# First row blocks' weights by ScalarE's queue, two products between mixed row blocks, mixing in accumulator banks

## The chip, the cores and the metric

The kernel runs on one core of one Trainium2 chip. The metric is the device time of one execution in microseconds (us); the number compared is the median of several runs. A profiled execution of the same kernel gives the page and the trace that this text reads. Engines are named as the profile names them: PE is TensorE's matmul, PEld its weight load, DVE is VectorE, ACT is ScalarE, POOL is GpSimd, SP is SyncE, which issues most of the transfers.

## The reference

Inputs are `x` (32 batches, 64 channels, 1024 positions), one condition number out of 16 for each batch, and a table of sixteen 64 x 64 mixing matrices. A two-layer network of width 4096 follows, and its result is added to `x`:

```python
W = weights[condition]                      # (32, 64, 64)
y = einsum('bct,bcd->bdt', x, W)            # mixing of channels, per batch
h = gelu(einsum('bsd,df->bsf', y, inter_w) + inter_b)
out = x + einsum('bsf,fd->bsd', h, output_w) + output_b
```

Everything is float32. The two matrix products of the network are the bulk of the work; the mixing is a small piece at the beginning.

## The kernel before

**Mixing.** Two batches make one row block of 128 partitions (2 x 64 channels); there are 16 row blocks. The function `mix` multiplies, for each of 8 slices of 128 positions and for each of the two batches, a 64 x 128 piece of `x` (the stationary operand) with the 64 x 64 weights of that batch. That is 16 matmul instructions, which the profile records as 32 matmuls and 32 weight loads, as each float32 instruction is executed in two passes. The results lie in PSUM, and `mixed` copies them into Y, the left operand of the network, half by ScalarE and half by VectorE. Tiles named `x` hold row blocks of the input, `wsel_e` their mixing weights, `py` the PSUM results. Ten row blocks are mixed before the products begin (in the order 2, 3, 6, 7, 0, 1, 4, 5, 8, 9), six more later, between products (tile `pl`, function `mix_later`).

**Weights of the mixing.** `start_rows` loads the condition numbers and works out a table row for each partition. `gather` then fetches the weights of one row block by an indirect transfer of GpSimd's queue; there are ten of these at the beginning.

**The products.** Both network products are done by two nested levels of a Strassen-Winograd scheme: seven products of quarter matrices (`OUTER`), each of them by seven products of quarters of those (`INNER`). An inner product is four matmul instructions (eight passes of 256 columns), accumulated in PSUM tiles of tags A, B and C, two buffers each (`psacc`). `product` issues it, `read` adds the result into SBUF tiles (`fX`, `fV`, `fD`). The operands other than plain quarters are sums: of the weights, by GpSimd (`outer_w1`, `inner_w1`), and of Y, by `right_sums`, in which ScalarE copies one operand into PSUM (pool `pst`, tag t) and VectorE adds. The first product of all, fA, takes block (0,0) of quarter 11 of Y and of the weights; the second, fB, takes block (1,0) of the same quarter of Y. Of Y both need only row blocks 0 and 1.

**Order.** Nothing is scheduled by a planner: each step is registered by `at(time, function)`, and all steps are issued in the order of these times, in units of one inner product. Each engine executes its instructions in that order. `MIX` is the distance of row blocks in these units. x is loaded into six buffers (`xpool`), so the seventh load waits for the first mixed block. SP issues first the condition numbers, then six row blocks of x, then the first quarter of the weights (`load_w1(0, "11")`), then four more row blocks as buffers come free, then the other three quarters of the weights.

**PSUM.** Before the products, mixing has its own pool `psx`, three buffers of two banks each; `end_mix` closes it and opens the accumulator pool in its place. `warm` fills TensorE's first microseconds with matmuls of zeros: 24 instructions of 256 columns.

Of the kernel before, what the change touches and what calls it, by code (L numbers as in the profile page):

```python
# [9 lines left out]
F32 = mybir.dt.float32  # L10
# [3 lines left out]
PSUM = bass.MemoryType.PSUM  # L14
# [8 lines left out]
LEFT = {1: "11", 2: "12", 3: "s4", 4: "22", 5: "s1", 6: "s2", 7: "s3"}  # L23
RIGHT = {1: "11", 2: "21", 3: "22", 4: "t4", 5: "t1", 6: "t2", 7: "t3"}
# [51 lines left out]
def kernel(  # L76
# [35 lines left out]
    nc = tc.nc  # L112
    P = 128
# [9 lines left out]
    W = 256  # L123
# [43 lines left out]
    row_c = early.tile([P, NR], I32, name="row_c")  # L167
    wsel_e = early.tile([P, NR - NL, D], F32, name="wsel_e")
    pst = ctx.enter_context(tc.tile_pool(name="pst", bufs=2, space=PSUM))
    psx_ctx = ctx.enter_context(ExitStack())  # L170
    psx = psx_ctx.enter_context(tc.tile_pool(name="psx", bufs=3, space=PSUM))
    late = {}

# [2 lines left out]
    def at(time, fn, *args):  # L178
        steps.append((time, len(steps), fn, args))
# [57 lines left out]
    def blk(q, a, b):  # L237

        return q[:, 2 * a : 2 * a + 2, ts(b, W)]

    def lblk(q, a, b):

        return blk(q, b, a)
# [15 lines left out]
    def wsel(i):  # L259
        return wsel_e[:, i, :] if i < NR - NL else wsel_l[:, i - (NR - NL), :]  # L260

    def gather(i):
# [4 lines left out]
            in_offset=bass.IndirectOffsetOnAxis(ap=rows[:, i : i + 1], axis=0),  # L267
        )


    XT = {}

    FIRST = (2, 3, 6, 7, 0, 1, 4, 5)

    def load_x(i):
        XT[i] = xpool.tile([P, T], F32, tag="x0", name=f"x0_{i}")
# [2 lines left out]
    def warm():  # L279


        z = misc.tile([P, 3 * P], F32, tag="m8", name="zeros")
        nc.vector.memset(z, 0.0)
        for n in range(2):
            t = psx.tile([P, 2, NK, D], F32, tag="py", name=f"warm{n}")
            t = t.rearrange("p j k d -> p (j k d)")
            for _ in range(12):
                nc.tensor.matmul(  # L288
                    t[:, :W], z[:, :P], z[:, P:], start=True, stop=True
                )  # L290

    Y = {}
    Y_ORDER = ("11", "21", "t2", "t3", "t4", "12", "22")
# [6 lines left out]
    YS = {}  # L300
    PY = {}

    def mix(i, out=None):
        if out is None:
            py = psx.tile([P, 2, NK, D], F32, tag="py", name=f"py{i}")
            out = [py[:, j] for j in range(2)]
        for k in range(NK):
            for j in range(2):
                half = slice(j * C, (j + 1) * C)
                nc.tensor.matmul(  # L310
                    out[j][:, k, :],
                    XT[i][half, ts(k, P)],
                    wsel(i)[half, :],
                    start=True,
                    stop=True,
                )
        PY[i] = out
# [22 lines left out]
        YS[i] = t[:, 1, :].rearrange("p (k n) -> p k n", k=NK)  # L340
        nc.sync.dma_start(XT[i], x_rows[i])

    def mix_later(i):
        tiles = [pst.tile([P, 2, W], F32, tag="t", name=f"pl{i}_{j}") for j in range(2)]
        mix(i, [t.rearrange("p a (k d) -> p (a k) d", d=D) for t in tiles])

    def mixed_later(i):
        for j in range(2):
            o = YS[i][:, :, ts(j, D)]
# [20 lines left out]

    def end_mix():
        x0.close()
        psx_ctx.close()
        late["yib"] = right1.enter_context(
            tc.tile_pool(name="yib", bufs=3, side="right", reuse_waits="tile")
        )
        late["acc"] = ctx.enter_context(
            tc.tile_pool(name="psacc", bufs=2, space=PSUM, reuse_waits="tile")
        )


    def outer_y0(a, b):
        return lambda: {
            n: blk(Y[0, n], a, b)
            for n in ("11", "12", "21", "22", "t1", "t2", "t3", "t4")
        }
# [26 lines left out]
    def inner_y(a, p):  # L413
        q = Y[a, RIGHT[p]]
        pool = yia if p in (1, 2) else late["yib"]
        t = lambda n: pool.tile([P, 2, W], F32, tag=f"yi{p}", name=f"y{n}_{a}_{p}")
        YI[a, p] = {
            "11": blk(q, 0, 0),
            "21": blk(q, 1, 0),
            "22": blk(q, 1, 1),  # L420
            "12": blk(q, 0, 1),
            "t1": blk(q, 0, 1),
            "t2": t("i2"),
            "t3": t("i3"),
            "t4": t("i4"),
        }
        return YI[a, p]
# [28 lines left out]
    def inner_w1(it, p):  # L456
# [21 lines left out]
            "s4": s4,  # L478
        }


    LAST = 7 * NH * NG - 1
    state = {}
# [28 lines left out]
    def plan_block(base, unit, blkno, key, nm, mm, operands):  # L512

        last = {}
        for q in INNER:
            slot = q[0]
            if blkno == LAST and slot == 11:
                slot = 7.5
            at(base + slot * unit, product, blkno, q, nm, mm, operands)
            at(base + (slot + 1) * unit, read, blkno, key, q, nm)  # L520
            last[q[4]] = base + (slot + 1) * unit
        return last
# [145 lines left out]
    at(-61, warm)  # L668
    at(-60, start_rows)
    order = FIRST + (8, 9)  # L670
    for j, i in enumerate(order):
        at(-50 + 0.1 * j, gather, i)
    for n in Y_ORDER:
        at(-45, new_y, 0, n)
    MIX = 1.15
    t0 = -len(order) * MIX - 0.7
    for j, i in enumerate(order):
        t = t0 + j * MIX
        at(-40 + 0.1 * j if j < 6 else t0 + (j - 6) * MIX + 1.5, load_x, i)
        at(t, mix, i)  # L680
        at(t + MIX + 0.4, mixed, i)
    at(t0 + 10 * MIX + 1, store_y1, 8)
    at(-39.45, load_w1, 0, "11")
    for j, n in enumerate(("12", "21", "22")):
        at(t0 + 3 * MIX + 1.6 + 0.1 * j, load_w1, 0, n)
    at(-1, lambda: nc.sync.dma_start(b1, inter_b.rearrange("(f p) -> p f", p=P)))
    at(t0 + 10 * MIX + 0.42, end_mix)
    ty = t0 + 4 * MIX + 1.5
    right_sums(ty, outer_y0(0, 1))
    right_sums(ty + 2.3, lambda: inner_y(0, 1))  # L690
    for j, (n, b) in enumerate(((0, 0), (1, 0), (1, 1))):
        right_sums(ty + 4.6 + 2.3 * j, outer_y0(n, b))
    right_sums(ty + 11.5, lambda: inner_y(0, 2))
    for j, p in enumerate((6, 7, 4, 5, 3)):
        right_sums(7 * (j + 2) - 4.5, lambda p=p: inner_y(0, p))
    later = (11.6, 13.9, 21.8, 26.2, 33, 46.6)
    for j, t in enumerate(later):
        i = NR - NL + j
        at(7.5 + 3 * j, gather, i)
        at(max(t - 6, later[j - 2] + 3.3 if j > 1 else 2), load_later, i)  # L700
        at(t, mix_later, i)
        at(t + 1.4, mixed_later, i)
        at(t + 3.2, store_later, i)

# [8 lines left out]
    for it in range(nit):  # L713
# [4 lines left out]
                at(b0 - 49 + t, load_w1, it, n)  # L718
        for n, t in W_AT.items():
            if it == 0:  # L720
                t = {1: -10, 2: -6.8, "s3": -4, "s1": -3}.get(n, t)
            if isinstance(n, str):
                at(b0 + t, outer_w1, it, n)
            else:
                at(b0 + t, inner_w1, it, n)
        for o, p in enumerate(OUTER):
            b = b0 + 7 * o
            plan_block(
                b, 1, 7 * it + o, (it, p), "f", mm1,
                lambda l, r, it=it, p=p, a=a: (WI[it, p][l], YI[a, p][r]),  # L730
            )
            fin = STATE[p][1]
            if fin is not None:
                hidden(b, it, fin)
            if it == NG:
                at(b - 49 + 13, load_y1, Y_ORDER[o])
                right_sums(b - 49 + 20, lambda p=p: inner_y(1, p), gap=0.8)
# [417 lines left out]
```

## Time and profile before

| what | value |
|---|---|
| median of three runs | 1366.71 us (1366.69 to 1367.29) |
| the profiled execution | 1367.58 us |
| its span on the core | 1365.8 us |
| PE busy | 1347.9 us, 99% of the span |
| mean granted clock of TensorE | 0.987 |
| first mixed block begins | 13.86 us |
| first product begins | 49.59 us |
| third product (the first fC) begins | 55.05 us (chain of waits) |

The span is the time from the first to the last instruction that the profile records; the profiled execution's own time is 1.8 us longer. Times of single instructions are counted from the start of the span. A line such as `PE py L310 x32` reads: TensorE, writing tile py, from line 310 of the kernel, 32 records. The granted clock is the share of its full clock that TensorE was given.

### The profile page before, as it was taken

To read this page: it belongs to the slowest core of one execution; us is meant where nothing else is said; L and a number is where in the kernel's file an instruction comes from. 1 tells how busy PE (TensorE), PEld (TensorE's weight loads), DVE (VectorE), ACT (ScalarE), POOL (GpSimd) and SP (SyncE) were. 2 spreads that over 40 slices of the span, in tenths; PEclk is the share of its full clock that TensorE was granted. 3 is DMA by queue.
4 is the path that set the end of the run, shared out by engine and by line. 5 is a ranking of instruction groups with operands and counts; after the bars stand their busy time and mean duration, and the time that the engine had idled before them with its cause. 6 is when DMAs were issued, how large, how long until landed. Compare 5 with 4: busy or idle time off the path is not lost.

```text
span 1365.8 us, 19025 instructions
## 1 busy us (share of the span) xinstructions
PE 1347.9 (99%) x6568; PEld 1182.9 (87%) x6568; DVE 883.3 (65%) x1581; ACT 488.9 (36%) x985; POOL 962.0 (70%) x601
## 2 busy tenths in 40 slices
PE   8999999999999999999999999999999999999998
PEld 8988888888888888888888888888888888888887
DVE  1656557565697665756657575675766757767676
ACT  1433324234354252532524332432433323333341
POOL 4762864957749678396672985958959689496792
PEclk7799999999999999999999999999999999999999
DMA  6455577676898767676668227074270732916611
GB/s 221 135 164 198 175 235 277 232 248 220 301 355 284 232 219 248 244 231 226 230 206 313 95 96 290 18 292 168 79 291 1 266 127 103 358 41 233 245 48 62
DMA packets 135216, 273.40 MB, mean 200 GB/s; under 512 B 15440, under 2 KB 67920, under 8 KB 123472
## 3 DMA queue, kind: packets, MB, share of 16 engines
q1 hardware_dynamic: 134336, 271.53, 57.4%
q8 instruction: 53, 0.87, 0.2%
q0 software_dynamic: 512, 0.53, 0.1%
q14 instruction: 43, 0.35, 0.1%
q10 hardware_dynamic: 272, 0.13, 0.0%
HBM read 167.28 MB, written 104.86 MB: 199 GB/s over the span
## 4 chain that ended last, share of the span: by engine, by line
PE 92%; DVE 4%; issue 1%; ACT 1%; POOL 1%; DMA 1%; DVEq 0%; ACTq 0%
PE fA L527 26%; PE zA L538 24%; PE fC L527 13%; PE zC L538 12%; PE fB L527 6%; PE zB L538 6%; PE py L310 2%; PE tp L1011 1%; DVE hs L187 1%; PE warm L288 1%; PE pl L310 1%; POOL w2p L187 1%; DVE fX L187 1%; DVE fV L187 0%; DMA hs_d<-fD 0%
## 5 line engine op out<-in xcount | busy, mean ns | idle before, releaser
L527 PE MATMUL fA<-yi,wi 128*128 128x256 f32 x896 | 212.5, 380 | 2.5 <-DVE fD L187 1.1
L187 DVE TENSOR_TENSOR hs<-h,t 128x512 f32<-128x512 f32 x308 | 200.5, 681 | 7.0 <-ACT t L207 2.9
L538 PE MATMUL zA<-hs,wt 128*128 128x256 f32 x840 | 197.8, 379 | 0.0
L187 POOL TENSOR_TENSOR h<-h,h 128x1024 f32<-128x1024 f32 x84 | 196.1, 2360 | 1.1 <-DMA h<-hs_d 0.9
L527 PEld LDWEIGHTS fA<-yi,wi 128*128 128x128 f32 x896 | 169.4, 190 | 28.1 <-DVE fX L187 1.9
L538 PEld LDWEIGHTS zA<-hs,wt 128*128 128x128 f32 x840 | 158.4, 190 | 20.9
L187 POOL TENSOR_TENSOR wi<-w 128x512 f32<-128x512 f32 x80 | 101.8, 1272 | 43.8 <-PE fC L527 24.5
L552 ACT ACTIVATE fD<-fD,b 128x256 f32<-128x256 f32 x128 | 58.2, 503 | 186.4 <-DVE fD L187 185.5
L187 POOL TENSOR_TENSOR ws<-w,w 128x1024 f32<-128x1024 f32 x32 | 74.8, 2359 | 68.6 <-PE fA L527 58.3
L207 ACT COPY t<-h 128x512 f32<-128x512 f32 x140 | 82.0, 591 | 74.2 <-DVE hs L187 69.9
L207 ACT COPY t<-hs 128x512 f32<-128x512 f32 x112 | 65.6, 589 | 108.5 <-DVE hs L187 108.5
L187 POOL TENSOR_TENSOR wt<-v 128x512 f32<-128x512 f32 x35 | 44.6, 1275 | 82.3 <-DMA v<-w_d 69.8
L187 DVE TENSOR_TENSOR fX<-fA,fX 128x512 f32<-128x512 f32 x104 | 71.6, 688 | 46.6 <-PE fA L527 46.5
L187 POOL TENSOR_TENSOR wi<-w,wi 128x512 f32<-128x512 f32 x40 | 50.9, 1273 | 63.8 <-PE fA L527 57.1
L527 PE MATMUL fC<-y,wi 128*128 128x256 f32 x384 | 91.0, 380 | 0.1
L527 PEld LDWEIGHTS fC<-y,wi 128*128 128x128 f32 x384 | 72.7, 190 | 10.4 <-issue 0.5
L538 PE MATMUL zC<-hs,v 128*128 128x256 f32 x336 | 79.5, 379 | 1.3 <-ACT mX L921 1.3
L527 PE MATMUL fA<-yi,w 128*128 128x256 f32 x320 | 75.6, 379 | 0.0
L538 PE MATMUL zA<-h,wt 128*128 128x256 f32 x320 | 75.6, 379 | 0.0
L538 PEld LDWEIGHTS zC<-hs,v 128*128 128x128 f32 x336 | 63.7, 190 | 10.2 <-ACT mX L921 1.7
L187 POOL TENSOR_TENSOR wt<-v,wt 128x512 f32<-128x512 f32 x35 | 44.5, 1272 | 33.7 <-PE zA L538 33.7
L538 PEld LDWEIGHTS zA<-h,wt 128*128 128x128 f32 x320 | 60.8, 190 | 8.3
(182 smaller groups left out, 2840.1 us busy)
## 6 DMA issues: line engine op xcount, KB each, us to landing
h<-hs_d SPq DMA_DIRECT2D x56, 1024.0 KB, 7.0
w<-in_L_ffn_inter_w_dram SPq DMA_DIRECT2D x32, 1024.0 KB, 6.8
hs_d<-hs SPq DMA_DIRECT2D x96, 256.0 KB, 3.1
v<-w_d SPq DMA_DIRECT2D x21, 1024.0 KB, 9.3
hs_d<-fD SPq DMA_DIRECT2D x64, 256.0 KB, 3.4
w2p<-in_L_ffn_output_w_dram SPq DMA_DIRECT2D x32, 512.0 KB, 5.0
w_d<-w2p SPq DMA_DIRECT2D x64, 256.0 KB, 2.8
w_d<-w2t SPq DMA_DIRECT2D x48, 256.0 KB, 6.7
```

What stands on the lines that cost most here:

```text
L187: eng.tensor_tensor(o, a, b, ALU.subtract if sub else ALU.add)
L207: nc.scalar.copy(t, src)
L288: nc.tensor.matmul(t[:, :W], z[:, :P], z[:, P:], start=True, stop=True)
L310: nc.tensor.matmul(out[j][:, k, :], XT[i][half, ts(k, P)], wsel(i)[half, :], start=True, stop=True,)
L527: nc.tensor.matmul(acc[:, u, :], lt[:, k, ts(u, P)], rt[:, k, :], start=start and u == 0 and k == 0, stop=k == 1, skip_group_check=True,)
L538: nc.tensor.matmul(acc, wl[:, k, :], hr[:, k, :], start=start and k == 0, stop=k == NG - 1, skip_group_check=True,)
L552: nc.scalar.activation(t[:, u, :], t[:, u, :], AF.Gelu_apprx_tanh, bias=b1[:, f : f + 1])
L1011: nc.tensor.transpose(tp[:, v, ts(n0, P)], d[:, n0, ts(v, P)], late["ident"])
```

## The change

Four things change together.

1. A new function `first_rows` fetches the mixing weights of row blocks 0 and 1. ScalarE loads the four condition numbers into registers and issues four transfers of 64 x 64 numbers, each at an address that a register gives. These two blocks are mixed first, and GpSimd gathers weights only from the third block on.
2. The first two products, fA and fB, are issued after the third mixed block, ahead of the other seven. Their operands are taken straight from Y and from the loaded weights (`y_block`, `w1_block`), as the sums are not made yet.
3. Mixing writes into the accumulator tiles of tags C and B in turn, two tiles for a row block. The pool `psx` is gone, and `mix_later` is merged into `mix`.
4. The warm-up is 26 instructions of 128 columns instead of 24 of 256. The first quarter of the weights is loaded after two row blocks of x instead of after six. The sums of Y come in another order (first those of quarter 11 itself, `inner_y(0, 1)`, then the outer ones), and one of them, t1, gets a tile of its own. Some times of later steps are shifted.

```diff
+    acc_pool = ctx.enter_context(tc.tile_pool(name="psacc", bufs=2, space=PSUM))
...
+    def first_rows(n):
+        _, idx = nc.values_load_multi_w_load_instructions(
+            cond[None, : 2 * n], engines=[mybir.EngineType.Activation],
...
+        for i in range(n):
+            for j in range(2):
+                nc.scalar.dma_start(
+                    wsel(i)[j * C : (j + 1) * C, :],
+                    cond_w[bass.ds(idx[2 * i + j], 1), :, :].rearrange("s c d -> (s c) d"),
+                )
...
-    FIRST = (2, 3, 6, 7, 0, 1, 4, 5)
+    NF = 2
+    FIRST = (0, 1, 2, 3, 6, 7, 4, 5)
...
-        for n in range(2):
-            t = psx.tile([P, 2, NK, D], F32, tag="py", name=f"warm{n}")
...
-            for _ in range(12):
+        t = acc_pool.tile([P, 2, W], F32, tag="A", name="warm")
+        for _ in range(26):
+            nc.tensor.matmul(t[:, 0, :P], z[:, :P], z[:, P:], start=True, stop=True)
...
-            py = psx.tile([P, 2, NK, D], F32, tag="py", name=f"py{i}")
+        pool = acc_pool if tag else pst
+        tiles = [
+            pool.tile([P, 2, W], F32, tag=tag or "t", name=f"py{i}_{j}") for j in range(2)
+        ]
...
+            if blkno == 0 and slot < 2:
+                slot += t0 - 2
...
+    at(-60, first_rows, NF)
-    for j, i in enumerate(order):
+    for j, i in enumerate(order[NF:]):
         at(-50 + 0.1 * j, gather, i)
-    MIX = 1.15
-    t0 = -len(order) * MIX - 0.7
+    MIX = 1.06
+    NB = 3
+    t0 = 2 - (len(order) - NB) * MIX
+    M_AT = {i: t0 + (j - NB) * MIX - (2 if j < NB else 0) for j, i in enumerate(order)}
...
+        at(t, mix, i, "CB"[j % 2])
...
-    at(-39.45, load_w1, 0, "11")
+    at(-39.85, load_w1, 0, "11")
...
+    right_sums(M_AT[3] + MIX + 0.5, lambda: inner_y(0, 1))
+    ty = M_AT[7] + MIX + 0.8
+    for j, (n, b) in enumerate(((0, 1), (1, 1), (0, 0))):
+        right_sums(ty + 2.3 * j, outer_y0(n, b))
+    right_sums(ty + 6.9, lambda: inner_y(0, 2))
+    right_sums(ty + 9.2, outer_y0(1, 0))
...
-    later = (11.6, 13.9, 21.8, 26.2, 33, 46.6)
+    later = (12.5, 14.3, 21.8, 26.2, 33, 46.6)
```

The order on TensorE is then: warm-up; row blocks 0, 1, 2; fA, fB; row blocks 3, 6, 7, 4, 5, 8, 9; the first fC and the rest of the products as before. On SP the order is: condition numbers, x of blocks 0 and 1, the first quarter of the weights, x of blocks 2, 3, 6 and 7, then 4, 5, 8 and 9 as buffers come free, then the other quarters of the weights.

## The prediction, made before the changed kernel was run

> **What bounds the kernel now.** I read the busy shares first, then the clock row of the slices, then the chain of waits from 0 to 60 us, then the windows on PE.
>
> ```profile
> PE 1347.9 (99%) x6568; PEld 1182.9 (87%) x6568; DVE 883.3 (65%) x1581; ACT 488.9 (36%) x985; POOL 962.0 (70%) x601
> ...
> PEclk7799999999999999999999999999999999999999
> ...
> q8 instruction: 53, 0.87, 0.2%
> ```
>
> TensorE is busy 99% of the span, so only less TensorE time, or a faster clock for it, can pay. The clock row has its only low digits in the first two slices (34 us each). The chain there is TensorE alone:
>
> ```profile
> 1.33 12.61 PE warm L288 x48
> 13.93 2.15 PE py L310 x35
> 16.08 1.12 issue
> 17.20 0.44 PE py L310 x3
> 17.64 1.67 issue
> 19.30 30.35 PE py L310 x281
> 49.66 3.67 PE fA L527 x8
> 53.32 1.73 PE fB L527 x8
> 55.05 1.73 PE fC L527 x8
> ```
>
> Warm-up to 13.9, one mixed row block (32 matmuls), a stop of 3.2 us, then nine blocks in 30 us, then the products. fA, the same work as fB, takes 3.67 against 1.73 us. The windows say why; columns are sum, busy us, clock, DMA share, GB/s:
>
> ```profile
> 13.90:16.00 2.10, 2.10 (x36) 1.00 0.65 215
> 16.10:19.30 3.20, 0.44 (x3) 0.96 0.09 26
> ...
> 25.80:29.20 3.40, 3.40 (x36) 0.50 0.49 154
> ...
> 46.30:49.60 3.30, 3.30 (x32) 0.50 0.00 0
> 49.60:53.20 3.60, 3.60 (x10) 0.51 0.43 147
> 53.20:54.90 1.70, 1.70 (x10) 1.00 0.95 283
> ```
>
> After the stop the clock is 0.50 and stays there through 30 us of unbroken mixing; it comes back only 3.5 us into the products. A block costs 3.41 us at 0.50 (ScalarE's copies of consecutive blocks start at 25.80 and 29.21). At 1.00 it costs 1.93: the first later block runs from 70.52 to 72.45 in the timeline. So about 9 x 1.48 = 13.3 us of the mixing, and 1.9 us of fA, are clock.
>
> **What the Trainium skill says.** "TensorE: Matmul & The Clock Gate", Part 1, has the clock halved after about one idle window of 3.4 us and restored after one busy window. The trace agrees on both steps (0.50 after the stop, 1.00 after 3.5 us of products), but adds that mixing matmuls, busy all the time on 64 of 128 rows, do not count as busy enough to restore it. Whether they count as idle enough to lose it from 1.00, neither says: before has no stretch of 3.4 us of mixing alone at 1.00. This is the open question. "Runtime: NRT & Kernel Launch", Instruction fetch mechanics, has blocks of 16 KiB, 256 instructions, fetched by DMA, and a stall after a branch. The trace agrees: queue 8 moved 0.87 MB in 53 packets, 16 KB each, and its first packet comes inside the stop[...].
>
> **The change part by part**, on TensorE's clock of before (span 1365.8, the profiled execution 1367.58, the median 1366.71; I sum differences on the profiled one and take them from the median, 0.9 us apart).
>
> Warm-up. 24 matmuls of 256 columns (48 passes) become 26 of 128 (52 passes of half size). At full clock eight passes of 256 take 1.73 us, so a half pass takes 0.108; at half clock 0.216. Before began at half rate too (6, 7, then 11 matmuls in the 2 us stretches from 2, 4 and 6 us), to about 5.4. Up to there 19 passes, then 33 x 0.108 = 3.6: the end is at 9.0 instead of 13.9.
>
> First weights. Gathers of POOL now serve blocks from the third on, at the times that the first had: issue at 5.06, landing at 10.2, then one each 1.25 us. Blocks 0 and 1 get theirs from ScalarE: two register loads, then four transfers of 16 KB. Before shows no such thing. "DMA: Bandwidth & Descriptors", Latency and other measured facts, has about 0.6 us as the floor of a register load; no run here shows it. Two of them after 0.74, four issues of 0.42 (SP's for x) and 3.3 to 4.7 to landing (x's own) give 5.7 to 8.4. If each load took 1.5 us: 10. I take 9.0, with no cost; bounds 0 and +3. The table load of ScalarE (1.28) now stands behind them, which costs nothing: its first copy is due at 11. x and w: block 0's x still lands at 5.9; w moves past four x loads and lands near 9.8. Later x loads on SP now wait for landings of ScalarE's transfers, as they share completion semaphores; at 390 GB/s they land one each 1.3 us, ahead of blocks of 1.9, so nothing is charged.
>
> Block 0: 9.0 to 10.9. Then the fetch stop. In before it came after 166 matmul and weight-load records (48 + 35 of each); now 104 + 64 = 168 lie ahead, so the same stop comes right after block 0. I take 3.3 us, to 14.2; bounds 0 and 5. The clock falls as in before. Blocks 1 and 2 at 0.50: 6.8, to 21.0. The two products (fA, fB, moved ahead of seven blocks) restore it, at before's price of 3.67 + 1.73 = 5.4: 26.4.
>
> Banks. Mixing now takes pairs of tiles of tags C and B, two buffers each, so block 3 needs fB read out first. Behind it on TensorE stand six blocks and all products; SP's last x load and the copies on ScalarE and VectorE wait along. Before's row:
>
> ```profile
> 55.16 0.69 DVE L187 TENSOR_TENSOR fX<-fB,fX 128x512 f32<-128x512 f32 x1 [1.44 <-PE fB L527]
> ```
>
> 0.11 + 0.69 + 0.1 = 0.9: to 27.3. Before had three buffers; blocks of 1.93 with two need copies within that time. ScalarE's pair (0.65) and VectorE's (0.76) fit, but sums of Y stand between them on both in-order queues; I charge 1.2 for all, bounds 0 and 3.
>
> Seven blocks at 1.00: 13.5. Sum 27.3 + 13.5 + 1.2 = 42.0 for the start of the first fC, which was at 55.05. **Gain 13.0 us: 1366.7 - 13.0 = 1353.7.** By kinds: warm-up -4.9, seven blocks x -1.48 = -10.4, new waits +2.1.
>
> What covers the rest. The other three w loads and POOL's sums follow block 3, so they stay near before's time (x's last load is issued at about 29, as before) while products come 13 us earlier. The last W sum was done at 55.8 and first used at 78.0; 65 now, 9 us of slack. Inner sums of it were done at 63.3, used at 81.4, now 68: 5 us. If that is gone, TensorE waits and gives back the excess. The inner Y sum for block 2 of products ends, by twelve VectorE operations of about 0.62, 7.4 to 8.5 us after the mixing and is needed at 12.1. The copy of t1 into its own tile, the reordered sums and the shifted later blocks cost TensorE nothing for the same reason. POOL issues two gathers less (1.25 each) ahead of its first W sum, which is due only after 27.
>
> **Rivals.**
> (A) as summed: the clock, restored by two products, holds through mixing. For it: windows of half mixing, half products (the later blocks from 70 to 80 us) keep 1.00. Against: nothing shows mixing alone at 1.00. 1353.7, own range 1350.5 to 1357.
> (B) Mixing alone loses the clock after about one window. Then of the seven blocks some 1.7 run at 1.93 and 5.3 at 3.41: 21.4, to 48.7 (slow blocks hide the copies), and the next product pays 1.9 again: 50.6 plus up to 2 for where the window falls. Gain 2.5 to 4.5, 1363.
> (C) The stop is shorter than a window and doesn't cost the clock: 2 x 1.48 + 1.9 = 4.9 more, 1348.8. For it: warm-up and block 0 stand close before. Against: before lost it there, in every run to judge by times within 0.6 us.
> (D) Slower: ScalarE's transfers are late. Block 0 heads TensorE's in-order queue, so everything waits for it, and an idle window costs the clock. It decides where (B) holds too: each us past 9.0 is lost, so (B)'s gain is gone at about 12.5, and the kernel is measurably slower from 15. With weights at 16.5: 1363 + 7.5 = 1370.5. Against: the first five gathers, the slowest transfers here, landed 5.1 to 5.5 us after issue; that would make 9 to 10.
> (E) The front is shorter but the slack above is not there, and TensorE waits for W sums until all is given back: 1365 to 1367.
>
> **How the numbers follow.** A 0.42, C 0.18, B 0.27, D 0.08, E 0.05. The likeliest is A, 1353.7. The range 1347.5 to 1365.3 takes in C, A and most of B and leaves out D and E. This kernel's measurement can tell about 0.2%, 2.7 us. Faster: A, C and 0.16 of B, 0.76. Same: the rest of B and E, 0.16. Slower: D, 0.08.
>
> **What would show it.** The first py matmul near 9 (later: D, with ScalarE's transfers as releaser); a stop of about 3 us after 32 py matmuls at a first 16 KB instruction packet (none: the fetch step is wrong); clock 0.50 for blocks 1 and 2 and back within the two products (1.00 throughout: C); seven blocks of about 2 us at 1.00 (3.4 us at 0.50: B); the first fC near 42; no new idle time of PE before POOL's sums from 50 to 100 us (E). If seven blocks run at 1.00 and the time is still above 1360, the reasoning on slack is wrong; if they run at 0.50, the reading of the clock is.

## The result and the profile after

| kernel | median | runs | lowest to highest |
|---|---|---|---|
| before | 1366.78 us | 20 | 1365.63 to 1367.36 |
| changed | 1363.84 us | 20 | 1356.37 to 1366.10 |

The ratio is 0.9969, with a 95% interval from 0.9957 to 0.9982: faster by 2.9 us, where 13.0 were forecast. The changed kernel's runs fall into two groups: six lie between 1356.4 and 1358.9 us, fourteen between 1362.9 and 1366.1. The profiled execution took 1365.32 us (span 1363.5), so it belongs to the second group; against the profiled execution of before its span is 2.3 us shorter.

The page of the changed kernel, the rows that answer to those of before:

```profile
PE 1340.6 (98%) x6572; PEld 1174.7 (86%) x6572; DVE 882.7 (65%) x1581; ACT 487.2 (36%) x985; POOL 959.7 (70%) x599
...
PEclk7999999999999999999999999999999999999999
```

The clock row has one low digit where before had two: TensorE's clock is back earlier, as intended. But PE is now busy 98% of the span, not 99%: there is idle time that was not there before. The timeline of PE of the changed kernel (start, us, then the group, in brackets idle time before it and what ended it) shows both:

```profile
11.21 2.22 PE L322 MATMUL py<-wsel_e,x 64*128 64x64 f32 x34 [1.03 <-DMA wsel_e<-in_L_cond_weights_dram]
...
15.08 1.19 PE L322 MATMUL py<-wsel_e,x 64*128 64x64 f32 x4 [0.45 <-issue]
16.50 5.82 PE L322 MATMUL py<-wsel_e,x 64*128 64x64 f32 x51 [0.24 <-issue]
22.25 3.78 PE L544 MATMUL fA<-y,w 128*128 128x256 f32 x8
...
29.18 13.30 PE L322 MATMUL py<-wsel_e,x 64*128 64x64 f32 x222 [0.49 <-DVE fX L186]
42.42 1.99 PE L544 MATMUL fC<-yi,wi 128*128 128x256 f32 x8
...
58.06 1.89 PE L544 MATMUL fC<-y,wi 128*128 128x256 f32 x8
65.17 3.68 PE L322 MATMUL py<-wsel_l,xl 64*128 64x64 f32 x32 [5.22 <-issue]
```

Up to the first fC all is nearly as summed: it begins at 42.42, where 42.0 was forecast and before has 54.89 in the same view (55.05 in the chain of waits). That is a lead of 12.5 us. Then, at the first of the later row blocks (line 322 with `wsel_l`), TensorE stands idle for 5.2 us, and that row block takes 3.68 us, not 2. The windows of the same kernel there (sum, busy us of PE, PEld, DVE, ACT and POOL with counts, clock, DMA share, GB/s):

```profile
62.00:64.00 2.00, 0.00 (x0) 0.00 (x0) 0.00 (x0) 0.00 (x0) 1.92 (x2) 1.00 1.00 387
...
66.00:68.00 2.00, 2.00 (x23) 2.00 (x22) 0.00 (x0) 0.00 (x0) 1.98 (x2) 0.50 0.08 25
...
70.00:72.00 2.00, 2.00 (x7) 1.61 (x7) 0.00 (x0) 0.24 (x1) 1.92 (x2) 0.64 0.54 165
```

The idle time takes the clock down to 0.50 from 64.6 to 71.4. In the 6.3 us of this in which TensorE works, half the work is done: 3.1 us more. A third piece is at 1269.5, one stretch of 3.4 us at 0.50 behind a wait of 2.2 us for VectorE, 1.7 us of work. Before has the same wait at the same place, but goes on at 1.00. PE's timelines there, the changed kernel first, then before:

```profile
1268.97 0.66 PE L1031 MATMUL tp<-ident,mY 128*128 128x128 f32 x4 [2.22 <-DVE xb L186]
1269.46 3.56 PE L555 MATMUL zC<-h,v 128*128 128x256 f32 x8
...
1273.15 0.66 PE L1011 MATMUL tp<-ident,mY 128*128 128x128 f32 x4 [2.22 <-DVE xb L187]
1273.64 1.89 PE L538 MATMUL zC<-h,v 128*128 128x256 f32 x8
```

So 12.5 - 5.2 - 3.1 - 1.7 = 2.5 us, where the spans differ by 2.3. The two groups of runs lie 7.0 us apart (medians 1357.7 and 1364.7), near the 5.2 + 3.1 of the late row block. But no profile of a shorter run on this chip was kept, and even the shorter runs gain only 9.1 us of the 12.5; what takes the rest there is open.

What TensorE waits for is `wsel_l`, the mixing weights of that row block; its x had landed by 52.5. The gather is POOL's. The timeline of POOL of the changed kernel:

```profile
40.34 1.27 POOL L186 TENSOR_TENSOR wi<-w 128x512 f32<-128x512 f32 x1 [20.22 <-DMA w<-in_L_ffn_inter_w_dram]
...
54.80 4.67 POOL L186 TENSOR_TENSOR ws<-w,w 128x1024 f32<-128x1024 f32 x2
59.63 0.96 POOL L262 DMA_INDIRECT wsel_l<-in_L_cond_weights_dram,rows  x1 [0.16 <-issue]
```

POOL waits 20 us for the three weight loads, then makes ten sums without a pause, 19.1 us, and only then issues the gather, though the gather needs nothing of these sums: it stands behind them in an in-order queue. It is issued at 59.63, 0.3 us before TensorE runs out of products, and its data are in 5.5 us later. SP had issued a weight load of 1 MB at 59.50, and the DMA engines move 387 GB/s meanwhile; in `r2_after` (below) the six such gathers were in after 2.3 to 3.2 us. So the wait is in part a late issue and in part a slow landing, and no run separates the two. POOL's timeline of before:

```profile
55.90 0.97 POOL L263 DMA_INDIRECT wsel_l<-in_L_cond_weights_dram,rows  x1
```

There the gather was in by 59.6 and used at 70.5. The change moved its use ahead by 10.6 us, and the gather itself back by 3.7, as POOL's first sum begins at 40.34 instead of 36.65.

### The profile page after: what moved, and what is told of

Read it like the earlier page. It is cut to its first block, busy times and chain, and to the rows that moved or that the text cites. A ratio compares the mean times of both kernels' runs of the same rounds, so it can differ in the third digit from the quotient of the medians.

```text
span 1363.5 us, 19040 instructions
## 1 busy us (share of the span) xinstructions
PE 1340.6 (98%) x6572; PEld 1174.7 (86%) x6572; DVE 882.7 (65%) x1581; ACT 487.2 (36%) x985; POOL 959.7 (70%) x599
## 4 chain that ended last, share of the span: by engine, by line
PE 53%; DVE 2%; POOL 1%; DMA 1%; issue 1%; ACT 1%; SPq 0%; DVEq 0%; ACTq 0%; POOLq 0%
PE zA L555 24%; PE zC L555 12%; PE zB L555 6%; PE fA L544 6%; PE fC L544 3%; PE fB L544 1%; PE tp L1031 1%; DVE hs L186 1%; DMA w2p<-in_L_ffn_output_w_dram 0%; POOL w2p L186 0%; POOL ws L186 0%; DVE mZ L186 0%; DVE mX L186 0%; ACT o L974 0%; DMA hs_d<-hs 0%
## 5 line engine op out<-in xcount | busy, mean ns | idle before, releaser
L186 POOL TENSOR_TENSOR wi<-w 128x512 f32<-128x512 f32 x80 | 101.8, 1272 | 50.1 <-PE fC L544 24.5
L186 DVE TENSOR_TENSOR fX<-fA,fX 128x512 f32<-128x512 f32 x104 | 71.4, 686 | 44.5 <-PE fA L544 44.4
L544 PE MATMUL fC<-y,wi 128*128 128x256 f32 x352 | 83.3, 380 | 0.1
L544 PEld LDWEIGHTS fC<-y,wi 128*128 128x128 f32 x352 | 66.7, 190 | 9.5 <-issue 0.5
L555 PEld LDWEIGHTS zC<-hs,v 128*128 128x128 f32 x336 | 63.7, 190 | 10.2 <-ACT mX L941 1.7
```

What stands on the lines that cost most here:

```text
L186: eng.tensor_tensor(o, a, b, ALU.subtract if sub else ALU.add)
L544: nc.tensor.matmul(acc[:, u, :], lt[:, k, ts(u, P)], rt[:, k, :], start=start and u == 0 and k == 0, stop=k == 1, skip_group_check=True,)
L555: nc.tensor.matmul(acc, wl[:, k, :], hr[:, k, :], start=start and k == 0, stop=k == NG - 1, skip_group_check=True,)
```

## The experiments

The kernel was run on several chips, and they differ in one point that matters here. In the first measurement, and in one later comparison (r4, e9, r3, e8), the kernel before takes 1366.7 us, with the stop that the prediction starts from. On five other chips it takes 1350.8 to 1352.1 us, and there is no such stop. I call them chips with and without the stop. Every ratio below is against the kernel before on the same chip, run alongside. The first expectations were written with 1366.7 in mind and name times that belong to a chip with the stop; what can be held against them on another chip is the part that speaks of waits and of the clock.

One table first, read from the traces of the profiled executions, as it carries most of what follows: start of the first fC, start of the first later row block, time at clock 0.50 up to 1340 us, and span, all in us.

| kernel | stop | first fC | first later block | at 0.50 | span |
|---|---|---|---|---|---|
| before | yes | 54.9 | 70.5 | 34.1 | 1365.8 |
| changed | yes | 42.4 | 65.2 | 23.9 | 1363.5 |
| before, `r1_before` | no | 37.8 | 53.5 | 0 | 1349.7 |
| changed, `r2_after` | no | 41.2 | 58.8 | 17.1 | 1355.1 |
| `e1_gather_early` | no | 41.6 | 59.3 | 17.1 | 1355.4 |
| `e2_before_gather_early` | no | 38.2 | 53.8 | 3.4 | 1350.6 |
| `e3_products_last` | no | 50.5 | 67.9 | 37.5 | 1361.5 |
| `e4_pool_weights` | no | 40.6 | 58.2 | 17.1 | 1354.1 |
| `e6_before_gap` | no | 56.8 | 72.5 | 37.5 | 1367.6 |
| `e7_long_warm` | no | 36.2 | 53.8 | 3.4 | 1349.9 |
| `x1_five_gathers` | no | 41.3 | 64.6 | 23.9 | 1362.2 |
| `x2_first_later_early` | no | 39.4 | 57.0 | 13.7 | 1353.2 |
| `x3_five_long_early` | no | 38.4 | 56.0 | 6.8 | 1351.7 |
| changed, `r4_after` | yes | 42.3 | 65.3 | 23.9 | 1363.5 |
| `e9_long_warm_alone` | yes | 42.4 | 64.0 | 20.5 | 1362.6 |
| `r3_long_warm` | yes | 50.1 | 67.7 | 20.5 | 1363.9 |
| `e8_pool_long_warm` | yes | 51.6 | 69.2 | 20.5 | 1365.1 |

### The later gathers early (e1, e2)

```diff
-        at(7.5 + 3 * j, gather, i)
+        at(-49 + 0.1 * j, gather, i)
```

In `e1_gather_early` this is done to the changed kernel, in `e2_before_gather_early` the same to before: all six later gathers go to the start of POOL's queue.

> The changed kernel with the gathers of the six later row blocks issued at the beginning, right behind the first eight, instead of between GpSimd's weight sums. Theory (queue): the changed kernel loses its gain because the gather of the first later block stands behind the weight sums on GpSimd's in-order queue (issued at 59.6, landed at 65.1, TensorE idle from 59.8 to 65.2 and then at half clock to 71.4). Then this stop is gone: the first later block follows the product at about 60, clock 1.00 there, and the time falls from 1363.8 by 5 to 9 us, to about 1355 to 1358. Rival (sums): the weight sums themselves are too late (my case E); then TensorE stops for them a few us later and the time stays above 1361. Rival (clock): the loss is clock that falls at one place or another whatever the order; then the time stays within 2 us of 1363.8.

> The kernel before with the same early gathers of the later row blocks. Theory (queue): in the kernel before these weights were issued at 55.9 and used at 70.5, so nothing waited for them: the same time as before within 0.7 us. Rival: early gathers are worth several us by themselves, by relieving GpSimd between the sums, whatever the rest: 1360 to 1363.

Measured, on a chip without the stop: e1 1355.85 us against 1352.12 (1.0024, 1.0014 to 1.0035); e2 1350.0 (0.9987, 0.9981 to 0.9994). In e1 TensorE waits only 0.36 us at the first later block, and that for a sum of Y. None of its ten runs is above 1357.2 us, while the changed kernel has long runs on a chip of this kind too (r2, below). So the late gather is the cause of the wait at 60 us. That e1's time lies in the expected 1355 to 1358 us is luck, as this was worked out for a chip with the stop.

e2 was expected within 0.7 us of before, and it is about 1.8 us faster. Before has a little of the same fault where there is no stop: in `r1_before` its second later block waits 1.00 us and begins at 60.11, when its gather has landed at 60.02. In e2 this wait is gone; where the rest of its gain lies was not traced.

But e1 is slower than before on this chip, which the theory had no place for. PE's timeline of e1 says why, in the first line; the second is the first later block:

```profile
11.05 0.40 PE L322 MATMUL py<-wsel_e,x 64*128 64x64 f32 x2 [1.99 <-DMA wsel_e<-in_L_cond_weights_dram]
...
60.06 2.00 PE L322 MATMUL py<-wsel_l,xl 64*128 64x64 f32 x30 [0.36 <-DVE yi L186]
```

The short warm-up ends at 9.1, the first weights are there at 11.05 and 11.8; the clock is 0.50 from 11.8 to 25.5. Before without the stop (`r1_before`) warms up to 14.4 and goes through its ten blocks without a wait.

### Both kernels again without the stop (r1, r2)

> The kernel before, unchanged, for a profile on the chip of these runs. In the first four experiments the kernel before took 1352.1 on their chip, against 1366.8 where the change was first measured. Theory (fetch stop): on such a chip TensorE doesn't stop after the first 166 records, so the clock never falls, ten blocks run at 1.93 or less, and the first fC begins near 38 instead of 55. Rival (elsewhere): the front is as in the first profile and the 14.7 us are saved later. If this chip is of the first sort, 1366.8 and the first profile again.

> The changed kernel, unchanged. Theory (queue, and clock from waiting): where the kernel before has no fetch stop, the change has nothing to win back; it still waits about 2 us for its first weights after a warm-up that ends at 9, loses the clock there, and stops at 59 to 65 for the gather of the first later block: 1361 to 1364 against 1352, slower by 0.7 to 0.9%. Rival: the change gains its 3 us on every chip: 1349. If this chip is of the first sort: 1363.8 as measured first.

Measured: before 1351.23 us; changed 1359.29 us (six runs, 1355.6 to 1363.8), ratio 1.0067 (1.0047 to 1.0088), where 1361 to 1364 was expected. **On this chip the change makes the kernel slower.** PE's timeline of before there:

```profile
14.32 18.08 PE L310 MATMUL py<-wsel_e,x 64*128 64x64 f32 x320
...
37.82 1.89 PE L527 MATMUL fC<-y,wi 128*128 128x256 f32 x8
```

Ten blocks in 18.1 us without a pause, at 1.00: the stop of 3.2 us and the 30 us at half clock, which the whole change is aimed at, do not exist here. Mixing alone for 18 us keeps the clock.

The profiled execution of the changed kernel there took 1356.9 us, so it is one of the shorter ones, and TensorE doesn't wait for the gather at the first later block (0.36 us, for a sum of Y). POOL's timeline, to be held against that of the changed kernel above:

```profile
36.58 1.27 POOL L186 TENSOR_TENSOR wi<-w 128x512 f32<-128x512 f32 x1 [16.40 <-DMA w<-in_L_ffn_inter_w_dram]
...
55.87 0.96 POOL L262 DMA_INDIRECT wsel_l<-in_L_cond_weights_dram,rows  x1
```

The same ten sums, the same 19.1 us, but begun 3.8 us earlier, as the weights were in earlier; the gather then comes in time, and PE begins the block at 58.81. So whether TensorE stands depends on a few microseconds of three weight loads. That would account for two groups of runs; that each long run has this wait and each short one not is inferred from three profiles with it (the changed kernel's first one, `r4_after`, `x1_five_gathers`; 1362 to 1363.5 us of span) and one without (1355.1). Why the loads, issued 1.2 us apart (31.6 and 30.4), land 3.8 us apart was not settled; the trace shows them moving at 206 to 233 GB/s over their first 4 us in the late case, at 366 to 392 in the early one.

### The products back behind all row blocks (e3)

e1 with all ten row blocks ahead of fA and fB:

```diff
-            if blkno == 0 and slot < 2:
-                slot += t0 - 2
...
-    M_AT = {i: t0 + (j - NB) * MIX - (2 if j < NB else 0) for j, i in enumerate(order)}
+    M_AT = {i: t0 + (j - NB) * MIX - 2.1 for j, i in enumerate(order)}
```

> The early-gather version of the changed kernel, but with all ten row blocks mixed first and fA and fB after them. Theory (products restore the clock): the clock falls at the fetch stop and nothing restores it during mixing, so seven more blocks run at 0.50, 7 x 1.48 = 10.4 us more than the early-gather version, about 1365. Rival (early start): the blocks run at full clock because the warm-up is shorter and mixing starts sooner; then it is within 2 us of the early-gather version.

Measured: 1363.32 us, 1.0081 (1.0068 to 1.0094), 7.5 us more than e1 on the same chip. PE's timeline of e3:

```profile
11.21 34.39 PE L322 MATMUL py<-wsel_e,x 64*128 64x64 f32 x318 [1.32 <-DMA wsel_e<-in_L_cond_weights_dram]
```

34 us of mixing at 0.50 once the clock is down (11.0 to 48.5), where e1 has it back after the two products. So the products do restore the clock, and mixing alone does not: the mechanism of the change is real wherever the clock has been lost. By the clock they are worth (37.5 - 17.1) / 2 = 10.2 us; at the first fC e3 is 8.9 us behind e1, at the end 7.5 by the medians and 6.1 by the profiled spans. 1.7 us of what it regains is a low stretch at 1261 that e1's profile has and e3's has not; the rest was not traced.

### ScalarE's transfers taken out (e4)

e1 with `NF = 0`: POOL gathers all ten.

> The early-gather version of the changed kernel without ScalarE's transfers: all ten first blocks get their weights by gathers of GpSimd's queue, in the same order of blocks. The first gather is issued at 5.06 and lands near 10.2; ScalarE's second half for block 0 landed at 10.9 in the changed kernel. Theory: ScalarE's transfers bring nothing, block 0 starts at 10.2 or a little later, the time is within 1.5 us of the early-gather version. Rival: they are what lets mixing start early; then block 0 starts 2 to 4 us later and so much is lost.

Measured: 1354.23 us, 1.0012 (1.0004 to 1.0020), 1.6 us less than e1, with intervals that overlap. The first block starts at 10.73 with POOL's gather, against 11.05 and 11.84 with ScalarE's transfers in e1. On a chip without the stop ScalarE's transfers bring nothing; they come no earlier than the gathers. In the trace of the changed kernel two register loads on ScalarE, of 0.88 and 2.33 us, stand ahead of them, so that the first is issued at 4.13, hardly before POOL's first gather (5.05 in e4). And a row block needs two of them: the second, issued at 4.87, was in only at 11.2. Why it takes so long was not tested.

### The stop built into before (e6)

Before with the gather of its second row block issued last of the ten:

```diff
-    for j, i in enumerate(order):
+    for j, i in enumerate(order[:1] + order[2:] + order[1:2]):
         at(-50 + 0.1 * j, gather, i)
```

> The kernel before with the gather of its second row block issued last of the ten (16.5 instead of 6.5), so TensorE stands idle some 3 to 4 us after the first block, as in the fetch stop. Theory (idle window): the clock falls to 0.50 and stays there through nine blocks; the time rises by the gap and 13.3 + 1.9, to 1367 to 1370 where before takes 1352. Rival (the gap alone): it costs itself, 1355 to 1356. On a chip with the fetch stop: within 2 us of before.

Measured, on a chip without the stop: 1368.98 us against 1351.36, 1.0130 (1.0115 to 1.0145). PE's timeline:

```profile
19.77 30.98 PE L310 MATMUL py<-wsel_e,x 64*128 64x64 f32 x288 [4.20 <-issue]
50.68 3.78 PE L527 MATMUL fA<-y,w 128*128 128x256 f32 x8
```

A wait of 4.2 us costs 17.6: nearly all the rest is the clock through nine blocks (0.50 from 18.4 to 56.0). This is the first chip's front, made on a chip that has none.

### The long warm-up (e7, and r3 on a chip with the stop)

e1 with 20 warm-up instructions of 256 columns, which end at 12.9:

```diff
-        for _ in range(26):
-            nc.tensor.matmul(t[:, 0, :P], z[:, :P], z[:, P:], start=True, stop=True)
+        for _ in range(20):
+            nc.tensor.matmul(t[:, 0, :], z[:, :P], z[:, P:], start=True, stop=True)
```

> The early-gather version of the changed kernel with 20 warm-up instructions of 256 columns instead of 26 of 128, so that warm-up ends near 11.5 and the first weights have landed. Theory (clock from waiting): no idle time between warm-up and mixing, no fall of the clock, blocks 0 to 2, fA and fB at full clock: 6 us less than the early-gather version (1355.9), 1347 to 1350. Rival (start counts): mixing starts later, so the time rises by 0 to 1 us. On a chip with the fetch stop the clock falls there anyway, and both are alike.

> The changed kernel with both edits: the long warm-up, and the gathers of the later row blocks issued at the start. Theory: neither cause of a low clock is left, so 1350.5 to 1352 whatever the chip; on a chip where the kernel before has its stop, the two products then bring the clock back by 28 us and it stays at or under 1356. Rival, that the later gathers did not matter: the same time as with the long warm-up alone.

Measured without the stop: 1351.35 us against 1351.36, 0.9999 (0.9991 to 1.0007), where 1347 to 1350 was expected. PE's timeline of e7:

```profile
12.88 5.58 PE L322 MATMUL py<-wsel_e,x 64*128 64x64 f32 x96
...
22.96 13.30 PE L322 MATMUL py<-wsel_e,x 64*128 64x64 f32 x222 [0.49 <-DVE fX L186]
```

No wait ahead of the first three blocks, clock 1.00, first fC at 36.2: a warm-up that ends 3.9 us later brings TensorE to the first fC 5.4 us earlier than in e1. The low clock of e1 came from the wait for the first weights.

The same kernel with the stop, where I expected at most 1356 us: **1364.96 us** against 1366.69, 0.9989 (0.9982 to 0.9996). This overturned my account of the stop as one fixed piece of 3 us. PE's timeline of `r3_long_warm`:

```profile
18.50 0.67 PE L322 MATMUL py<-wsel_e,x 64*128 64x64 f32 x3 [1.20 <-issue]
...
25.75 4.01 PE L322 MATMUL py<-wsel_e,x 64*128 64x64 f32 x32 [0.17 <-DVE y L347]
```

From 14 to 25.7 PE gets one to four matmuls at a time, with "issue" before each: it waits for nothing that the profile shows. The windows of the same kernel:

```profile
18.00:20.00 2.00, 0.77 (x4) 0.78 (x4) 0.00 (x0) 0.00 (x0) 1.56 (x2) 0.50 0.13 33
...
26.00:28.00 2.00, 2.00 (x20) 2.00 (x21) 0.72 (x3) 0.20 (x1) 1.61 (x2) 0.50 0.81 303
```

VectorE and ScalarE stand too, and almost nothing is moved; only POOL works. What POOL does is in the instructions of its gather line (count, ns, first and last start):

```profile
L262 POOL DMA_INDIRECT wsel_e<-in_L_cond_weights_dram,rows x8: 944/944/1102, 5.0 to 13.9; - x8
L262 POOL DMA_INDIRECT wsel_l<-in_L_cond_weights_dram,rows x6: 940/944/945, 15.2 to 21.4; - x6
```

Fourteen gathers, the last issued at 21.4 and landed at 23.4. In all six profiles with the stop, TensorE flows again within 2.5 us of the time at which the last gather's data are in (times read from the transfers in the trace):

| kernel (with the stop) | gathers at the start | last one landed | SP's queue moves nothing | PE flows again |
|---|---|---|---|---|
| changed | 8 | 17.1 | 15.8 to 17.7 | 16.5 |
| `r4_after` | 8 | 17.0 | 15.8 to 17.6 | 16.5 |
| `e9_long_warm_alone` | 8 | 16.1 | 15.8 to 17.6 | 16.4 |
| before | 10 | 19.3 | 15.3 to 20.5 | 19.3 |
| `r3_long_warm` | 14 | 23.4 | 15.8 to 25.9 | 25.7 |
| `e8_pool_long_warm` | 16 | 26.1 | 15.4 to 28.7 | 28.6 |

On chips without the stop, e7 (14 gathers) and e4 (16) keep mixing through the same time.

### Three more kernels with the stop (r4, e9, e8)

`r4_after` is the changed kernel; `e9_long_warm_alone` has the long warm-up only; `e8_pool_long_warm` is `r3_long_warm` without ScalarE's transfers.

> The changed kernel as it is. If this chip has the stop of some 3 us in the first row blocks of the kernel before (which is then near 1366), it stands a few us under it; if not (the kernel before near 1351), 3 to 10 us over it, in two groups: near 1356 where the gather of the first later row block is issued by about 56 us, near 1363 where it is issued near 59.6 and TensorE stands idle for about 5 us behind it.

> The changed kernel with 20 warm-up instructions of 256 columns in place of 26 of 128, and nothing else. Theory: the low clock of the first blocks comes from waiting for the first weights, so it goes, and some 4.5 us with it, against the changed kernel; but TensorE then reaches the later row blocks some 5 us earlier still, while their gather stays behind the W sums, so the stop there comes in more executions or is longer: it gives back up to 5 us of idle time and up to 3.4 us of clock. So between 1351 and 1361, in two groups. Rival: the weights' stream moves up with TensorE and the stop does not grow: 1351 to 1353 throughout.

> The same without ScalarE's transfers: all ten row blocks' weights by POOL's gathers, as in the kernel before; what is left of the change is the two products between the blocks and the accumulator banks. Theory: ScalarE's transfers bring nothing once the warm-up is long, so the same as with them, or up to 1 us less. Rival: with them the second block's weights come earlier and TensorE waits less: 1 to 2 us more without them.

Measured, against 1366.69: r4 1364.32 us, 0.9973 (0.9959 to 0.9986), which repeats the result, again with four of 15 runs lower, between 1355.3 and 1360.2; e9 1363.96 us, 0.9980 (0.9973 to 0.9987), all of its 20 runs between 1362.5 and 1364.7; e8 1366.90 us, 1.0005 (0.9996 to 1.0014). I was wrong that e8 would equal r3 or beat it: with the stop, taking ScalarE's transfers out, and so having two gathers more, makes it 1.9 us slower, and its first fC 1.5 us later. So ScalarE's transfers have a use on such a chip, though another than an early start: it fits two gathers fewer, and a shorter stop. e9 expected the low clock of the first blocks to go; with the stop it stays, as TensorE still pauses between 15.4 and 16.4, and it waits 4.05 us for the late gather (gather issued at 58.25, block begun at 64.02). It stays outside the expected 1351 to 1361 us, and in one group.

### Fewer gathers, and the first later one early (x1, x2, x3; y1, y3, y4)

`x1_five_gathers` gives ScalarE the last five of the ten row blocks, `x2_first_later_early` moves one later gather, `x3_five_long_early` does both, with the long warm-up:

```diff
-    at(-60, first_rows, NF)
-    for j, i in enumerate(order[NF:]):
+    at(-60, first_rows, order[5:])
+    for j, i in enumerate(order[:5]):
...
-        at(7.5 + 3 * j, gather, i)
+        at(7.5 + 3 * j if j else -49, gather, i)
```

> The changed kernel with five of the ten first row blocks by ScalarE's transfers in place of two (blocks 7, 4, 5, 8, 9, the last five of the order; POOL gathers the first five). Theory: on a chip where the kernel before has its stop (then near 1366.7), what stops there is everything that needs new instructions or a transfer while POOL's gathers are under way, from about 15.5 us until the last gather's packets are in: 17.6 us with 8 gathers, 20.5 with 10, 25.9 with 14, 28.6 with 16. Five gathers are in by about 14, so there is no stop at all: SP's queue has no pause from 15.5 and TensorE none at its 180th matmul. The clock still falls where the warm-up ends ahead of the first weights. So about 1356 to 1359, with the gather of the later blocks issued near 56 us. Rival: the stop is one of instruction supply at a fixed place in the program, and stays some 2 us whatever POOL does: 1363 to 1365 as with two. Where the kernel before is near 1351 there is no stop, and the run tells nothing of it: 1355 to 1364.

> The changed kernel with the gather of the first later row block alone moved to the start, behind the eight. Theory: TensorE's 5 us of idle time at that row block go, and the low clock behind it (3.4 us); on a chip with the stop, the ninth gather makes the stop 1.5 us longer: 1357 to 1359 in every execution there, against 1364 for the changed kernel. On a chip without it: 1355 to 1357, without a second group. Rival: the second later block's gather, now the first behind the W sums, is late in its place: a gain of under 3 us.

> Both edits, and 20 warm-up instructions of 256 columns: six gathers at the start, five row blocks by ScalarE. Theory: no stop, no wait for the first weights, no late gather, so the clock stays at 1.00 from the first window on: 1350 to 1352 on either kind of chip, 14 to 16 us under the kernel before where that has its stop. Rival: ScalarE's ten transfers come too late for the sixth block (needed by about 22 us), TensorE waits and the clock falls: 1356 or more.

The chip was one without the stop (before 1351.13 us). x2: 1355.07 us, 1.0030 (1.0023 to 1.0038), no run above 1357.2, so the second group is gone with this one gather. x1, which leaves it behind the sums, still has both groups (seven runs from 1354.3 to 1356.7, four from 1361.8 to 1364.3; median 1356.65, 1.0044, 1.0024 to 1.0064), and its profile, of a long run, shows the wait again, with POOL's gather issued at 59.07:

```profile
64.59 3.68 PE L322 MATMUL py<-wsel_l,xl 64*128 64x64 f32 x32 [5.76 <-issue]
```

So the late gather does not need the front's stop. x3: 1353.70 us, 1.0016 (1.0007 to 1.0024), where 1350 to 1352 was expected: the third block waits 1.06 us behind a copy of VectorE, and the clock falls for 3.4 us.

Whether the gathers cause the front's stop could be decided by x1 or x3 on a chip that has it. x3 was run three times more:

> The kernel with five row blocks by ScalarE, the long warm-up and one later gather early, again, for a chip with the stop (the kernel before near 1366.7). There, theory: its six early gathers are in by 14 us, before TensorE and SP's queue come to stand, so neither has the pause that ended at 17.6 us with 8 gathers and 25.9 with 14: 1352 to 1355, 12 to 14 us under the kernel before. Rival: the stop is tied to the place in the program and stays 2 us or more: 1358 to 1365, TensorE pausing between its 160th and 200th matmul. On a chip without the stop: 1352 to 1356 against 1351, as before, and nothing is told apart.

`y3_five_long_early` and `y4_five_long_early` had the same expectation. All three ran on chips without the stop: 1353.73 us (1.0012, 1.0006 to 1.0019), 1353.74 (1.0009, 0.9999 to 1.0018) and 1353.65 (1.0014, 1.0007 to 1.0021). In their profiles the third block waits 0.69, 1.22 and 0.62 us, and each time the clock falls for 3.4 us. They tell nothing of the stop. **It stays open** whether the gathers cause it, what makes a chip show it, and what x3 is worth there. No version was shown to beat both kernels on both kinds of chip: e2 is 0.13% under before where there is no stop and was not run with it.

## Why the prediction was wrong

**Right: what two products do for the clock.** The question that the prediction left open, whether mixing alone keeps a clock of 1.00, is answered with yes: 13.3 us in the changed kernel, 18.1 in before without the stop. Rival B is out, and A's mechanism stands: without the two products in between, the clock stays at 0.50 for 34 us of mixing (e3), with them it is back after 13.7 (e1).

**Right by errors that cancelled: the path to the first fC.** 42.42 measured, 42.0 summed. The warm-up ended at 9.8, not 9.0, since the clock rose at 6.6 and not 5.4; in r2 and e1 it ended at 9.0 and 9.1. ScalarE's first weights were taken at 9.0 and held block 0 until 11.2: the two register loads took 0.88 and 2.33 us, where I had taken the cited floor of 0.6 each and at most 1.5 each. The Trainium skill's "Runtime: NRT & Kernel Launch", The ~15µs preamble/postamble breakdown, gives register loads some 1.3 us; the second one here is above that too. So block 0 began 2.2 us late, inside the bounds given. The stop, taken as 3.3 us right after block 0, ran from 13.4 to 16.5 and let nine matmuls through. The two products took 6.0 us, not 5.4, as the clock came back only at 27.1, during the second. Against that, the seven blocks took 13.3 us with no copy in their way, where 13.5 + 1.2 was charged. The wait for the readout of fB was 0.9 as charged (28.3 to 29.2).

**Wrong: "the shifted later blocks cost TensorE nothing for the same reason".** This is the step that failed: a term put at nothing. The prediction followed POOL's sums to their users and found 9 and 5 us of slack. But on the same queue, behind the same sums, stands the gather of the first later row block, and its slack was not worked out. At before's times it would have been 0.4 us: the gather was in by 59.6, and TensorE now needs it at 59.95.

A second sentence failed with it, that the weight loads and the sums "stay near before's time". Block 3 was mixed about 2 us later than summed. SP's last load of x waits for it, so that it was issued at 31.2 and not "at about 29, as before", and the weight loads behind it at 31.6 instead of 29.6. POOL's first sum then began 3.7 us later than in before, and the gather was issued 3.7 us later. The late gather cost 5.2 us of idle time and 3.1 us of clock, 8.3 of the 13. e1 and x2 removed the wait by moving that gather, on chips without the stop.

The rival for a lost slack, E, named the wrong data (the sums) and gave the mechanism 0.05. The prediction also left out that a wait of 5 us costs the clock in addition, though it had used just that rule for the front.

**In no step: the 1.7 us at 1269.5.** The wait behind which they lie is in before too; what differs is where it falls. Within each of the 20 profiles the changes of the clock stand on one grid of 3.41 us (`r1_before` has only one change, at its end). In the changed kernel they lie at 13.41, 27.06, 64.61, 71.44 and 1269.52, that is 4, 11, 2 and 351 steps apart, and every low stretch before the end is a whole number of steps long. The wait of 2.2 us for VectorE is in every profile. In fifteen of them at least 2.06 us of it lie in one step, and the clock falls. In the other five, both profiles of before among them, the grid divides it, at most 1.77 us lie in one step, and the clock stays at 1.00. This is read from the traces; no run was made to move the wait along the grid.

**Wrong premise: the stop as a property of the kernel.** It was read as an instruction fetch after 166 to 168 records, 3.3 us long within bounds of 0 and 5. The records fit, but the length did not: from TensorE's first pause until it flows again it was 1.0 to 3.1 us with eight gathers, 3.2 with ten, 11.5 and 14.1 with 14 and 16, and there was none on five chips. The Trainium skill's "Runtime: NRT & Kernel Launch", Instruction fetch mechanics, calls the cost of crossing a 16 KiB boundary "mostly hidden"; the runs without the stop agree, and those with it do not, if the stop is such a crossing. That several engines stand at once, with "issue" as their only reason, speaks for the supply of instructions; that POOL's gathers hold it up is an inference from the table above.

**Rival D in part.** Late first weights were given 0.08 and a threshold of 12.5 us. They came at 11.2 on the chip with the stop, where little was lost by it: e9, which mixes from 12.7 on without having waited, reaches its first fC at the same 42.4. Without the stop the same lateness, a wait of 2 us, puts 13.7 us at 0.50; without this wait (e7 against e1) the ratio to before falls from 1.0024 to 0.9999, some 3.4 us. The Trainium skill's "TensorE: Matmul & The Clock Gate", Part 1, has the clock fall after about one idle window of 3.4 us; here waits of 2.0, 1.06 and 0.62 us beside mixing were enough (e1, x3, y4); that it also matters where a wait falls, the grid above shows.

## What to carry to other kernels

When a change brings one engine forward by several microseconds, list every transfer that it will need in the next tens of microseconds, and for each of them what stands before it in the queue that issues it; a tiny gather behind 19 us of unrelated sums is as late as the sums are. Price each new wait twice, as idle time and as the clock that it costs behind it, and where no other stop follows, let a warm-up last until the first operands have landed, even if it could end sooner. A front part that is bound by a stop with no visible releaser should be looked at on a second chip before a kernel is changed for it.

## What was not expected of the hardware

- One program has two times on different chips of one kind, 1366.7 and 1351 us, 1.1% apart, from a pause of about 3 us in its first 20 us and the clock that this costs.
- With that pause TensorE, ScalarE, VectorE and SP's queue stand together until about the time at which POOL's last early indirect transfer is in (8, 10, 14 and 16 gathers: SP's queue moves again at 17.7, 20.5, 25.9 and 28.7 us).
- The clock changes only on a grid of 3.41 us within a profile; the same wait of 2.2 us cost it in fifteen profiles, where it lay in one step, and not in five, where the grid divided it.
- Mixing on 64 of 128 rows keeps a clock of 1.00 for at least 18 us, and does not bring it back from 0.50 in 34.
- An indirect transfer of one row block was in 2.3 to 3.2 us after issue in `r2_after`, and 5.5 us after it beside a weight load at 387 GB/s.
- Loading addresses into ScalarE's registers took 2.1 to 2.3 us for four of them (changed kernel, r2, r4, e9) and 5.9 to 6.2 us for twelve (x1, x3, y1, y3, y4).
